# Last MLP, gates, selection and experts in one stage: four batches at a time, outputs added up in two PSUM banks

## The chip, the cores and the metric

The kernel runs on one core of a Trainium2 chip. The metric is the device time of one execution in microseconds (us); the median of three runs is given. The work is done by five engines with queues of their own: TensorE (PE, matmuls into PSUM), VectorE (DVE), ScalarE (ACT), GpSimd (POOL) and SyncE (SP, which issues the DMAs here).

## The reference

The network is a chain of eight blocks on `x` of 16 batches x 256 tokens x 128 features: four times an attention (or a scan) and a feed-forward block, each with a layer norm ahead of it and one on its output, and a residual addition. Only the end matters here: the last MLP of the block `L3_attn`, and the block `L3_ffn`, a mixture of experts in which each expert chooses its tokens.

```python
xa = xa + a_mlp_scale * (jnp.square(relu(rms_norm(xa) @ a_fc_w)) @ a_proj_w)   # last MLP
x = x + _layernorm(xa)
# L3_ffn on _layernorm(x): 8 experts, k = 64 tokens for each of them in each batch
probs = softmax(x @ gate_w).transpose(0, 2, 1)
g, m = top_k(probs, 64)
h = gelu(einsum('nekd,edf->nekf', x[m], w1)); h = einsum('nekf,efd->nekd', h, w2)
out = zeros.at[m].add(g[..., None] * h)            # scattered back to the tokens, bfloat16
x = x + _layernorm(out)
```

(The program text has `n` = 4 and `t` = 512 as constants, but takes both from the shape of `x`: 16 batches of 256 tokens, `k` = 64.)

## The kernel before

The 16 batches are held as eight groups `x[g]` of two batches, 128 tokens on the partitions, `[128, 4, 128]`, in float32. The program (L1778) is a row of stages. Each opens a pool for its work tiles on the left side of SBUF and its own PSUM pool; weights lie in pools on the left or right. All DMAs are issued from SP. A stage is written as Python generators, one for each group or unit, that `yield` between steps; `interleave` (L218) runs at most `depth` of them at a time and starts the next when the one before has made `lead` steps; `turns` (L372) starts each generator at a turn given for it. This sets the order in which instructions are written down. Where a stage isn't under `manual_schedule` (the attention and scan stages are), a scheduler then reorders the instructions of each engine and gives out the buffers of each tag as they come free. At run time each engine takes its instructions in the order so fixed, and waits on semaphores.

The end of the program is two stages:

- `stage_l3_last` (L1632), depth 4 and lead 2: for each of the eight groups the last MLP (`l3_mlp`, L1426: RMS norm, four transposes, four up matmuls of 512 columns, square of the ReLU on ACT and DVE, sixteen down matmuls), the residual with a layer norm (`residual`, L280; the statistics on DVE, the power -0.5 on POOL at L244), and `choice_gate` (L1645: layer norm into `exn`, four transposes, the gate's four matmuls of 8 columns, softmax over 8 experts with Exp on ACT at L1662, probabilities written to `probs` by POOL at L1668).
- `stage_choice_moe` (L1671): one selection for all 16 x 8 = 128 rows (batch, expert) of 256 probabilities: two transposes, then eight times the eight largest (`max`) and their replacement (`match_replace`) on DVE, the mask of the chosen, transposes back, three matmuls for the rank of each chosen token, `slot`. Then `pair_of(half, pair)`, for each half (eight batches) and each pair of experts, at depth 2: for each batch a one-hot matrix `hot` (DVE, L1722) and the same times the probabilities, `back` (POOL, L1724); a matmul gathers the tokens with `hot`; a transpose of `back` makes `put`; four up matmuls of 512 columns and a Gelu for each expert (L1744); down matmuls, 32 for each four batches (two experts side by side in the array); the outputs are copied to `y`. `put` and `y` of all four pairs are kept (6 buffers each). Behind the last pair of a half, for each group, 16 matmuls add up `put` x `y` over the four pairs in one PSUM bank; then `ob` (bfloat16), the layer norm, the addition on POOL and the output DMA.

PSUM in both stages is four tags of two banks: `BANKS = {"mm": 2, "s": 2, "o": 2, "t": 2}`. `copy` (L232) gives copies to DVE and ACT by turns. The pools around it: the l3 weights `wc` on the left (opened L1856), the experts' weights `wd` on the right (L1873).

Of the kernel before, what the change touches and what calls it, by code (L numbers as in the profile page):

```python
# [24 lines left out]
AF = mybir.ActivationFunctionType  # L25
ALU = mybir.AluOpType
# [1399 lines left out]
def l3_mlp(k, x, fc, proj, bufs=3):  # L1426

    n = yield from k.rmsnorm(x, "n", 3)
    yield
    nT = k.transposed(n, "nT", 3)  # L1430
    yield
    h = k.t([P, 4, GT], "mlp_h", 3)
    for i in range(4):
        ps = k.ps("s")
        k.mm(ps, fc[:, i * P : (i + 1) * P], nT)
        r = k.t([P, GT], "mlp_r", bufs)
        k.nc.scalar.activation(r, ps, AF.Relu)
# [191 lines left out]
        k.turns(items + [(at[-1] - 5, rotate())])  # L1629


def stage_l3_last(k, x, xm, w, rows, then):  # L1632


    def last(g):
        yield from l3_mlp(k, xm[g], w["afc"], w["aproj"])
        yield
        yield from k.residual(x[g], xm[g])
        yield
        yield from then(g)  # L1640

    k.interleave([last(g) for g in range(NG)], 4, 2)


def choice_gate(k, x, g, w, xn, probs):  # L1645


# [20 lines left out]
        nc.gpsimd.tensor_copy(probs[:, :, at : at + ne], p[:, 2 * b : 2 * b + 2, :])  # L1668


def stage_choice_moe(k, x, w, xn, probs, out):  # L1671

    nc, v = k.nc, k.nc.vector
    ident, ones = k.c["ident"], k.c["ones"]
    ne, cap = 8, 64

    ps = k.ps("t")
    for t in range(2):  # L1680
        nc.tensor.transpose(ps[:, t * P : (t + 1) * P], probs[:, t, :], ident)  # L1681
    cur = k.t([P, SEQ], "top", 2)
    v.tensor_copy(cur, ps[:, :SEQ])
    for _ in range(cap // 8):
        best = k.t([P, 8], "best", 2)
        v.max(out=best, in_=cur)
        nxt = k.t([P, SEQ], "top", 2)
        v.match_replace(out=nxt, in_to_replace=best, in_values=cur, imm_value=-1.0)
        cur = nxt
    chosen = k.t([P, SEQ], "chosen", 1)  # L1690
    v.tensor_scalar(chosen, cur, 0.0, None, ALU.is_lt)
    ps = k.ps("t")
    for t in range(2):
        nc.tensor.transpose(ps[:, t * P : (t + 1) * P], chosen[:, t * P : (t + 1) * P], ident)  # L1694
    mk = k.t([P, 2, P], "mk", 1)
    v.tensor_copy(mk, ps[:, :SEQ].rearrange("p (t r) -> p t r", t=2))

    rank = k.ps("s")[:, :SEQ].rearrange("p (t r) -> p t r", t=2)
    k.mm(rank[:, 0, :], k.c["before"], mk[:, 0, :])
    k.mm(rank[:, 1, :], ones, mk[:, 0, :], True, False)  # L1700
    k.mm(rank[:, 1, :], k.c["before"], mk[:, 1, :], False, True)
    slot = k.t([P, 2, P], "slot", 1)
    v.scalar_tensor_tensor(slot, rank, 1.0, mk, ALU.add, ALU.mult)
    v.tensor_scalar(slot, slot, -1.0, None, ALU.add)


    iota = k.c["iota"].rearrange("p (e c) -> p e c", e=2)
    puts, ys = {}, {}

    def pair_of(half, pair):  # L1710
        b0 = 8 * half
        put = puts[half, pair] = k.t([P, 8, SEQ], "put", 6)
        y = ys[half, pair] = k.t([P, 8, D], "ey", 6)
        xinT = k.t([P, 8, P], "xinT", 2)
        for i0 in range(0, 8, 4):
            xin = k.ps("o").rearrange("p (b c) -> p b c", b=4)
            for i in range(i0, i0 + 4):
                b = b0 + i
                r = b * ne + 2 * pair
                hot = k.t([P, 2, P], "hot", 4)  # L1720
                by_expert = hot.rearrange("p t (e c) -> p t e c", e=2)
                v.tensor_tensor(by_expert, bc(iota, 1, 2), bc(slot[:, :, r : r + 2], 3, cap), ALU.is_equal)  # L1722
                back = k.t([P, 2, P], "back", 4)
                nc.gpsimd.tensor_tensor(  # L1724
                    back.rearrange("p t (e c) -> p t e c", e=2), by_expert, bc(probs[:, :, r : r + 2], 3, cap), ALU.mult
                )
                for t in range(2):
                    k.mm(xin[:, i - i0, :], xn[b // 2][:, 2 * (b % 2) + t, :], hot[:, t, :], t == 0, t == 1)
                tp = k.ps("t")
                for t in range(2):  # L1730
                    nc.tensor.transpose(tp[:, t * P : (t + 1) * P], back[:, t, :], ident)  # L1731
                k.copy(put[:, i, :], tp[:, :SEQ])
                if i % 2:
                    yield
            k.copy(xinT[:, i0 : i0 + 4, :], xin)
        yield
        hs = []
        for j in range(2):
            w1 = w[f"w1_{2 * pair + j}"]
            h = k.t([P, 4, GT], "mlp_h", 3)  # L1740
            for f in range(4):
                ps = k.ps("s")
                k.mm(ps, w1[:, f * P : (f + 1) * P], xinT[:, :, j * cap : (j + 1) * cap])
                nc.scalar.activation(h[:, f, :], ps, AF.Gelu_apprx_tanh)  # L1744
                if f % 2:
                    yield
            hs.append(h)
        for i0 in range(0, 8, 4):
            ps = k.ps("mm").rearrange("p (b d) -> p b d", b=4)
            for i in range(i0, i0 + 4):  # L1750
                for f in range(4):
                    for j in range(2):
                        rows = slice(j * cap, (j + 1) * cap)
                        w2 = w[f"w2_{2 * pair + j}"].rearrange("p (c n) -> p c n", c=4)
                        k.mm(ps[rows, i - i0, :], hs[j][:, f, i * cap : (i + 1) * cap], w2[:, f, :], f == 0, f == 3)
            k.copy(y[:, i0 : i0 + 4, :], ps)
            yield
        if pair < 3:
            return
        for g in range(b0 // 2, b0 // 2 + 4):  # L1760
            ps = k.ps("o").rearrange("p (t d) -> p t d", t=NT)
            for n in range(NT):
                i, t = 2 * g + n // 2 - b0, n % 2
                for p in range(4):
                    k.mm(
                        ps[:, n, :], puts[half, p][:, i, t * P : (t + 1) * P], ys[half, p][:, i, :], p == 0, p == 3
                    )
            ob = k.t([P, NT, D], "ob", 3, dt=BF16)
            nc.scalar.copy(ob, ps)
            yield  # L1770
            yield from k.residual(x[g], ob)
            nc.sync.dma_start(out=out[2 * g : 2 * g + 2].rearrange("b (t p) d -> p (b t) d", p=P), in_=x[g])

    k.interleave([pair_of(half, pair) for half in range(2) for pair in range(4)], 2, 6)


@with_exitstack
def program(ctx: ExitStack, tc: tile.TileContext, xin, dram, at, out):  # L1778
    nc = tc.nc
# [42 lines left out]
    k = Ctx(tc, const, None, None)  # L1822
# [42 lines left out]
    with pool("first", "left") as pf:  # L1865
        first = []
        stage("l3m", "left", stage_trunk, l2, rows1["l2b2"], l3, rows3, lm, xm, first, pf, banks=MAMBA_BANKS)
        closed("lm")
        closed("wb")
        with phase("l3g", RING_BANKS):  # L1870
            l3_gqa(k, xm, l3, l3["gain"], first)

    pd = opened("wd", "right")  # L1873
    moe = load(pd, "moe")
# [5 lines left out]
    closed("wc")  # L1880
    stage("l3f", "left", stage_choice_moe, moe, en, probs, out)
    closed("wd")

# [19 lines left out]
```

## Time and profile before

| | |
|---|---|
| median of 3 runs | 3027.43 us (3027.18 to 3029.25) |
| the profiled execution's own time | 3030.76 us |
| its span, first to last instruction | 3029.1 us |
| busy: PE / DVE / ACT / POOL | 2758.7 / 1984.5 / 1602.5 / 1013.6 us |
| mean granted clock of TensorE | 0.956 |
| last MLP and gates (stage `l3q`) | 2689 to 2809.6 us |
| selection | 2809.6 to 2822.9 us |
| experts, first gather to last down matmul | 2822.9 to about 3004.5 us |
| last sums, norms and output | to 3029.1 us |

Lines of the profile name an engine, a line of the code, an operation, and the tiles written and read. L316 is the helper of all matmuls, so there the tile tells which one it is. "PEclk" is the share of full speed that TensorE's clock was granted. In the chain of work that ended last each line is a start in us, a duration in us, an engine and what it did, with the number of records; "issue" is time in which an engine waited for nothing that the profile shows.

### The profile page before, as it was taken

How to read it: one execution, taken by the hardware profiler on the slowest of the kernel's cores; microseconds unless marked ns; L12 is line 12 of the kernel's file. 1: busy time of each engine (PE TensorE's matmuls, PEld its weight loads, DVE VectorE, ACT ScalarE, POOL GpSimd, SP SyncE). 2: the span in 40 equal slices, each digit the busy share in tenths (PEclk: the TensorE clock that was granted, in tenths of full speed). 3: DMA queues.
4: the chain of work that ended last, by engine and by line, in shares of the span. 5: the costliest groups of instructions: out<-in, count | busy, mean ns of one | idle time of the engine just before them, and what ended most of it. 6: DMA issues, size and time to landing. Idle time of an engine off the chain costs nothing. (4 is left out here: it accounts for less than half of the span.)

```text
span 3029.1 us, 59064 instructions
## 1 busy us (share of the span) xinstructions
PE 2758.7 (91%) x23516; PEld 1855.1 (61%) x23516; DVE 1984.5 (66%) x5375; ACT 1602.5 (53%) x3372; POOL 1013.6 (33%) x1368
## 2 busy tenths in 40 slices
PE   8879999999997799999959997899999699978798
PEld 4547766767765588888834443566666344435576
DVE  5667465574657899999676773666655677637432
ACT  6745556455563577777615664444443377632222
POOL 3553333333336100000044553322322466553232
PEclk9989999999998899999979998999999799988899
DMA  4000000000000000000010000000000000010000
GB/s 114 11 1 2 1 2 2 1 2 1 2 5 33 4 12 8 8 8 9 19 62 1 1 2 1 1 2 1 1 1 2 1 1 1 2 56 1 1 15 15
DMA packets 29147, 31.26 MB, mean 10 GB/s; under 512 B 7292, under 2 KB 20156, under 8 KB 28732
## 3 DMA queue, kind: packets, MB, share of 16 engines
q1 hardware_dynamic: 28872, 27.49, 3.0%
q8 instruction: 185, 3.03, 0.4%
q14 instruction: 90, 0.74, 0.1%
HBM read 23.29 MB, written 4.19 MB: 9 GB/s over the span
## 5 line engine op out<-in xcount | busy, mean ns | idle before, releaser
L243 POOL TENSOR_SCALAR ln_rs<-ln_mv 128x4 f32<-128x4 f32 x192 | 39.8, 207 | 858.3 <-DVE ln_mv L256 836.8
L439 DVE TENSOR_REDUCE at_nm<-ps_s 128x2 f32<-128x512 f32 (+1 forms) x384 | 238.3, 682 | 124.2 <-PE ps_s L316 124.2
L471 ACT ACTIVATE at_e<-ps_s 128x512 f32<-128x512 f32 x384 | 198.2, 603 | 93.2 <-PE ps_s L316 91.1
L1390 DVE TENSOR_TENSOR scan<-ps_s,lm 128x384 f32<-128x384 f32 x256 | 124.8, 550 | 143.1 <-PE ps_s L316 142.8
L477 POOL TENSOR_SCALAR_AFFINE_SELECT at_e<-at_e 128x1024 f32<-128x1024 f32 (+1 forms) x96 | 135.4, 1411 | 215.5 <-ACT at_e L471 215.2
L244 POOL TENSOR_TENSOR ln_rs<-ln_rs,mhalf 128x4 f32<-128x4 f32 x192 | 195.8, 1020 | 15.7
L853 DVE TENSOR_REDUCE l_max<-ps_s 128x3 f32<-128x384 f32 x256 | 124.1, 549 | 64.0 <-PE ps_s L316 64.0
L316 PE MATMUL ps_o<-my,meT 128*128 128x129 f32 x1024 | 145.5, 289 | 18.4 <-ACT mgot L1147 15.4
L316 PEld LDWEIGHTS ps_s<-l_w,mlp_h 128*128 128x128 f32 x1280 | 149.4, 192 | 18.8 <-issue 15.1
L316 PE MATMUL ps_s<-l1f_phi,mxT 128*128 128x256 f32 x512 | 141.4, 398 | 16.9 <-DVE mpart L1009 16.7
L316 PE MATMUL ps_s<-km,qT 32*128 32x512 f32 x768 | 141.5, 666 | 11.9 <-POOL km L363 10.5
L316 PEld LDWEIGHTS ps_o<-my,meT 128*128 128x128 f32 x1024 | 128.6, 196 | 37.1 <-ACT mgot L1147 21.9
L316 PE MATMUL ps_s<-l_w,mlp_h 128*128 128x128 f32 x1280 | 150.2, 275 | 0.3
L316 PE MATMUL ps_s<-qm,kT 32*128 32x512 f32 x768 | 143.4, 652 | 5.2 <-DVE at_nm L439 5.0
L903 POOL TENSOR_SCALAR_AFFINE_SELECT e<-e 128x512 f32<-128x512 f32 x128 | 78.8, 637 | 178.3 <-ACT e L900 178.3
L316 PE MATMUL ps_o<-at_e,at_vm 128*32 128x128 f32 (+1 forms) x2048 | 123.4, 338 | 15.3 <-ACT at_oT L501 15.3
L316 PE MATMUL ps_mm<-mdisp,mxn 128*128 128x128 f32 x1024 | 125.2, 278 | 5.0 <-DVE mdisp L1047 4.9
L316 PEld LDWEIGHTS ps_mm<-mdisp,mxn 128*128 128x128 f32 x1024 | 121.7, 195 | 7.9 <-DVE mdisp L1047 6.6
L900 ACT ACTIVATE e<-ps_s 128x384 f32<-128x384 f32 x256 | 105.5, 510 | 39.7 <-PE ps_s L316 39.6
L316 PE MATMUL ps_s<-xT,l_w 128*128 128x512 f32 x256 | 119.3, 596 | 2.7 <-ACT mlp_h L788 2.7
L1367 ACT COPY BT<-ps_s 128x512 f32<-128x512 f32 x64 | 37.5, 586 | 154.6 <-PE ps_s L316 154.6
L316 PEld LDWEIGHTS <-b_ident 128*128 128x128 bf16 x656 | 51.3, 98 | 110.1 <-issue 100.0
(428 smaller groups left out, 7040.8 us busy)
## 6 DMA issues: line engine op xcount, KB each, us to landing
mw<-in_l1fw SPq DMA_DIRECT2D x16, 256.0 KB, 2.6
moe_w<-in_moe SPq DMA_DIRECT2D x16, 256.0 KB, 5.3
l_w<-in_l SPq DMA_DIRECT2D x10, 256.0 KB, 3.1
x<-in_x SPq DMA_DIRECT2D x8, 256.0 KB, 4.4
xs<-x SPq DMA_DIRECT2D x8, 256.0 KB, 2.0
slT<-xs SPq DMA_DIRECT2D x8, 256.0 KB, 2.6
out<-x SPq DMA_DIRECT2D x8, 256.0 KB, 2.3
l1f_phi<-in_l1f SPq DMA_DIRECT2D x1, 1024.0 KB, 5.0
```

Source lines behind the costliest of these rows:

```text
L243: g.tensor_scalar(out, in_, scale, eps, ALU.mult, ALU.add)
L244: g.tensor_tensor(out, out, self.mhalf[:, :n], ALU.pow)
L316: self.nc.tensor.matmul(out, lhsT=lhsT, rhs=rhs, start=start, stop=stop, skip_group_check=True)
L439: v_.tensor_reduce(nm[:, t, r, vs], s, AX.X, ALU.max, negate=True)
L471: nc.scalar.activation(e[:, r], s, AF.Exp)
L477: nc.gpsimd.affine_select(at, at, [[0, 4], [0, n], [1, P]], ALU.is_ge, 0.0, base=0, channel_multiplier=-1)
L853: v.tensor_reduce(mx[:, b, :, h, 16], s, AX.X, ALU.max, negate=True)
L900: nc.scalar.activation(e[:, h].rearrange("p j n -> p (j n)"), s[:, : 3 * P], AF.Exp)
L903: nc.gpsimd.affine_select(e[:, :, j, :], e[:, :, j, :], [[0, 4], [1, P]], ALU.is_ge, 0.0, base=0, channel_multiplier=-1)
L1367: nc.scalar.copy(s, ps)
L1390: v.tensor_tensor(m, s[:, : SEQ + P], lm[:, SCAN_HEADS[4 * (t // 2) + 2 * i + hh], :], ALU.mult)
```

## The change

The two stages become one, `stage_last`, which starts its generators by turns:

- `last(g)`: MLP, residual and gate of a group, as before, started every two turns for the first six groups, the last two at turns 16 and 20;
- `selection(q)`, q = 0 to 3: the selection of one quarter (four batches, 32 rows of 256), at turns 15, 19, 23 and 36;
- `pair_of(q, pair)`: one pair of experts for four batches, one every three turns from turn 21. An up matmul has 256 columns instead of 512, two of them share a bank and a Gelu. The outputs of a pair are added at once, in eight matmuls, into two PSUM banks that stay open over the four pairs (`sums`, one bank for each of the quarter's two groups), so `put` and `y` of a pair are free after it (4 and 3 buffers).

PSUM becomes one ring of six banks for everything, and two for the sums. `mlp_r` in the MLP has 2 buffers instead of 3. The l3 weights go to the right side, the two of the last MLP (`afc`, `aproj`) in a pool of their own, loaded first; the l2 weights' pool `wb` stays open to the end.

In the changed program the instructions of each engine stand as before up to the start of the l2 attention, where VectorE's casts of `att_sel` and `att_rows` come before the first norm instead of after the first maxima; from there they are equal up to the last stage. On SP the l3 weights, which stood behind the eight reloads `slT<-xs` of the soft stage, stand between them. In the last stage ScalarE has five table loads (Gelu, Exp, Gelu, Exp, Gelu), where it had one: the gates of the last two groups stand between Gelus. TensorE and VectorE stand so, in outline:

```
TensorE: MLP of groups 0 to 5, gates 0 to 4 and selection 0 among them; MLP of group 6;
  gathers of (0,0) with the up matmuls of group 7; selection 1; (0,0) with gathers of (0,1); gate 6;
  sums of (0,0); gathers of (0,2); selection 2; ... then one (q, pair) after the other
VectorE: MLP, norms and gates of groups 0 to 4, nearly all of 5, n and mlp_h of 6; selection 0;
  four hot; selection 1, group 6; four hot; selection 2, group 7; hot of (0,2) ...
```

The diff (`-` and `+`; its core):

```diff
+LAST_BANKS = {"s": 6, "sum": 2, "mm": "s", "t": "s"}
...
-    k.interleave([last(g) for g in range(NG)], 4, 2)
...
-def stage_choice_moe(k, x, w, xn, probs, out):
+def stage_last(k, x, xm, w, xn, probs, out):
...
+    def last(g):
+        yield from l3_mlp(k, xm[g], w["afc"], w["aproj"], 2)
+        yield
+        yield from k.residual(x[g], xm[g])
+        yield
+        yield from choice_gate(k, x, g, w, xn, probs)
+
+    def selection(q):
+        rows = nb * ne
+        ps = k.ps("s")
+        for t in range(2):
+            nc.tensor.transpose(ps[:rows, t * P : (t + 1) * P], probs[:, t, rows * q : rows * (q + 1)], ident)
+        cur = k.t([rows, SEQ], "top", 2)
+        v.tensor_copy(cur, ps[:rows, :SEQ])
+        for n in range(cap // 8):
+            best = k.t([rows, 8], "best", 2)
+            v.max(out=best, in_=cur)
+            nxt = k.t([rows, SEQ], "top", 2)
+            v.match_replace(out=nxt, in_to_replace=best, in_values=cur, imm_value=-1.0)
+            cur = nxt
+            if n % 2:
+                yield
...
-    def pair_of(half, pair):
-        b0 = 8 * half
-        put = puts[half, pair] = k.t([P, 8, SEQ], "put", 6)
-        y = ys[half, pair] = k.t([P, 8, D], "ey", 6)
-        xinT = k.t([P, 8, P], "xinT", 2)
+    def pair_of(q, pair):
+        put = k.t([P, nb, SEQ], "put", 4)
+        y = k.t([P, nb, D], "ey", 3)
+        xinT = k.t([P, nb, P], "xinT", 2)
...
+        h = k.t([P, 2, 4, SEQ], "mlp_h", 3)
         for j in range(2):
             w1 = w[f"w1_{2 * pair + j}"]
+            for f in (0, 2):
+                ps = k.ps("s")
+                for u in range(2):
+                    at = (f + u) * P
+                    k.mm(ps[:, u * SEQ : (u + 1) * SEQ], w1[:, at : at + P], xinT[:, :, j * cap : (j + 1) * cap])
+                nc.scalar.activation(
+                    h[:, j, f : f + 2, :], ps.rearrange("p (u n) -> p u n", u=2), AF.Gelu_apprx_tanh
+                )
+            yield
...
+        if pair == 0:
+            sums[q] = [k.ps("sum").rearrange("p (t d) -> p t d", t=NT) for _ in range(2)]
+        for u, o in enumerate(sums[q]):
+            for n in range(NT):
+                i, t = 2 * u + n // 2, n % 2
+                k.mm(o[:, n, :], put[:, i, t * P : (t + 1) * P], y[:, i, :], pair == 0 and n == 0, pair == 3)
         if pair < 3:
             return
...
-    k.interleave([pair_of(half, pair) for half in range(2) for pair in range(4)], 2, 6)
+    items = [(2 * g if g < 6 else 4 * g - 8, last(g)) for g in range(NG)]
+    for q in range(4):
+        items.append(((15, 19, 23, 36)[q], selection(q)))
+        items += [(21 + 12 * q + 3 * pair, pair_of(q, pair)) for pair in range(4)]
+    k.turns(items)
...
-    pc = opened("wc", "left")
-    l3 = load(pc, "l3")
+    pe = opened("we", "right")
+    last = load(pe, "l3", {"afc", "aproj"})
+    pc = opened("wc", "right")
+    l3 = load(pc, "l3", set(at["l3"]) - set(last))
+    l3.update(last)
...
-    gate = lambda g: choice_gate(k, x, g, moe, en, probs)
-    stage("l3q", "left", stage_l3_last, xm, l3, rows3, gate)
+    stage("last", "left", stage_last, xm, last, en, probs, out, banks=LAST_BANKS)
...
-    stage("l3f", "left", stage_choice_moe, moe, en, probs, out)
```

More of the change, by code (lines that the diff above doesn't have):

```diff
@@ L1629, in stage_trunk @@
         k.turns(items + [(at[-1] - 5, rotate())])
[L1632 to L1640, printed above, removed]
-    k.interleave([last(g) for g in range(NG)], 4, 2)
 def choice_gate(k, x, g, w, xn, probs):
@@ L1668, in choice_gate @@
         nc.gpsimd.tensor_copy(probs[:, :, at : at + ne], p[:, 2 * b : 2 * b + 2, :])
-def stage_choice_moe(k, x, w, xn, probs, out):
+def stage_last(k, x, xm, w, xn, probs, out):
     nc, v = k.nc, k.nc.vector
     ident, ones = k.c["ident"], k.c["ones"]
[L1677 to L1704, printed above, removed]
-    iota = k.c["iota"].rearrange("p (e c) -> p e c", e=2)
-    puts, ys = {}, {}
-    def pair_of(half, pair):
-        b0 = 8 * half
-        put = puts[half, pair] = k.t([P, 8, SEQ], "put", 6)
-        y = ys[half, pair] = k.t([P, 8, D], "ey", 6)
-        xinT = k.t([P, 8, P], "xinT", 2)
[L1715 to L1735, printed above, removed]
-        yield
-        hs = []
@@ new lines, in stage_last @@
+    ne, cap, nb = 8, 64, 4
+    iota = k.c["iota"].rearrange("p (e c) -> p e c", e=2)
+    slots, sums = {}, {}
+    def last(g):
+        yield from l3_mlp(k, xm[g], w["afc"], w["aproj"], 2)
+        yield
+        yield from k.residual(x[g], xm[g])
[16 more added lines that the diff above has]
+                yield
+        chosen = k.t([rows, SEQ], "chosen", 1)
+        v.tensor_scalar(chosen, cur, 0.0, None, ALU.is_lt)
+        ps = k.ps("s")
+        for t in range(2):
+            nc.tensor.transpose(ps[:, t * rows : (t + 1) * rows], chosen[:, t * P : (t + 1) * P], ident[:rows, :rows])
+        mk = k.t([P, 2, rows], "mk", 2)
+        v.tensor_copy(mk, ps[:, : 2 * rows].rearrange("p (t r) -> p t r", t=2))
+        rank = k.ps("s")[:, : 2 * rows].rearrange("p (t r) -> p t r", t=2)
+        k.mm(rank[:, 0, :], k.c["before"], mk[:, 0, :])
+        k.mm(rank[:, 1, :], ones, mk[:, 0, :], True, False)
+        k.mm(rank[:, 1, :], k.c["before"], mk[:, 1, :], False, True)
+        slot = slots[q] = k.t([P, 2, rows], "slot", 3)
+        v.scalar_tensor_tensor(slot, rank, 1.0, mk, ALU.add, ALU.mult)
+        v.tensor_scalar(slot, slot, -1.0, None, ALU.add)
+        yield
@@ new lines, in pair_of @@
+    def pair_of(q, pair):
+        put = k.t([P, nb, SEQ], "put", 4)
+        y = k.t([P, nb, D], "ey", 3)
+        xinT = k.t([P, nb, P], "xinT", 2)
+        xin = k.ps("s").rearrange("p (b c) -> p b c", b=nb)
+        for i in range(nb):
+            b, r = nb * q + i, i * ne + 2 * pair
+            hot = k.t([P, 2, P], "hot", 4)
+            by_expert = hot.rearrange("p t (e c) -> p t e c", e=2)
+            v.tensor_tensor(by_expert, bc(iota, 1, 2), bc(slots[q][:, :, r : r + 2], 3, cap), ALU.is_equal)
+            back = k.t([P, 2, P], "back", 4)
+            at = b * ne + 2 * pair
+            nc.gpsimd.tensor_tensor(
+                back.rearrange("p t (e c) -> p t e c", e=2), by_expert, bc(probs[:, :, at : at + 2], 3, cap), ALU.mult
+            )
+            for t in range(2):
+                k.mm(xin[:, i, :], xn[b // 2][:, 2 * (b % 2) + t, :], hot[:, t, :], t == 0, t == 1)
+            tp = k.ps("s")
+            for t in range(2):
+                nc.tensor.transpose(tp[:, t * P : (t + 1) * P], back[:, t, :], ident)
+            k.copy(put[:, i, :], tp[:, :SEQ])
+            if i % 2:
+                yield
+        k.copy(xinT, xin)
+        yield
+        h = k.t([P, 2, 4, SEQ], "mlp_h", 3)
@@ L1738, in pair_of @@
         for j in range(2):
             w1 = w[f"w1_{2 * pair + j}"]
-            h = k.t([P, 4, GT], "mlp_h", 3)
-            for f in range(4):
[L1742 to L1757, printed above, removed]
+            for f in (0, 2):
+                ps = k.ps("s")
+                for u in range(2):
[3 more added lines that the diff above has]
+                    h[:, j, f : f + 2, :], ps.rearrange("p (u n) -> p u n", u=2), AF.Gelu_apprx_tanh
+                )
@@ new lines, in pair_of @@
+            yield
+        ps = k.ps("s").rearrange("p (b d) -> p b d", b=nb)
+        for i in range(nb):
+            for f in range(4):
+                for j in range(2):
+                    rows = slice(j * cap, (j + 1) * cap)
+                    w2 = w[f"w2_{2 * pair + j}"].rearrange("p (c n) -> p c n", c=4)
+                    k.mm(ps[rows, i, :], h[:, j, f, i * cap : (i + 1) * cap], w2[:, f, :], f == 0, f == 3)
+        k.copy(y, ps)
+        yield
+        if pair == 0:
+            sums[q] = [k.ps("sum").rearrange("p (t d) -> p t d", t=NT) for _ in range(2)]
@@ L1758, in pair_of @@
+        for u, o in enumerate(sums[q]):
+            for n in range(NT):
+                i, t = 2 * u + n // 2, n % 2
+                k.mm(o[:, n, :], put[:, i, t * P : (t + 1) * P], y[:, i, :], pair == 0 and n == 0, pair == 3)
         if pair < 3:
             return
[L1760 to L1767, printed above, removed]
+        for u, o in enumerate(sums[q]):
+            g = 2 * q + u
@@ L1768, in pair_of @@
             ob = k.t([P, NT, D], "ob", 3, dt=BF16)
-            nc.scalar.copy(ob, ps)
+            nc.scalar.copy(ob, o)
             yield
@@ L1868, in program @@
         closed("lm")
-        closed("wb")
         with phase("l3g", RING_BANKS):
             l3_gqa(k, xm, l3, l3["gain"], first)
+    closed("wc")
     pd = opened("wd", "right")
-    moe = load(pd, "moe")
+    last.update(load(pd, "moe"))
     en = [pd.tile([P, NT, D], F32, tag=f"exn{g}", name=f"exn{g}") for g in range(NG)]
     probs = pd.tile([P, 2, NB * 8], F32, tag="probs", name="probs")
-    gate = lambda g: choice_gate(k, x, g, moe, en, probs)
-    stage("l3q", "left", stage_l3_last, xm, l3, rows3, gate)
+    stage("last", "left", stage_last, xm, last, en, probs, out, banks=LAST_BANKS)
+    closed("wd")
+    closed("we")
+    closed("wb")
     closed("xm")
-    closed("wc")
-    stage("l3f", "left", stage_choice_moe, moe, en, probs, out)
-    closed("wd")
 def kernel(**inputs):
```

## The prediction

> **What bounds the kernel now.** I read the page's slices first, to see which stretch the change touches; then the windows view by stage; then the chain of work that ended last; then the costliest groups by form for that stretch.
>
> ```profile
> PE   8879999999997799999959997899999699978798
> ...
> DVE  5667465574657899999676773666655677637432
> ...
> PEclk9989999999998899999979998999999799988899
> ```
>
> Slice 36 onwards (a slice is 75.7 us) is the part from 2689 us to the end: TensorE falls to 7 and 8 where its neighbours have 9. The windows view cuts this part by stage (last MLP, selection, experts, tail), then the MLP stage more finely:
>
> ```profile
> core 0: us, PE busy (x) PEld busy (x) DVE busy (x) ACT busy (x) POOL busy (x), PEclk, DMA share, GB/s
> 2689.00:2809.60 120.60, 87.94 (x448) 61.63 (x448) 80.33 (x296) 25.20 (x48) 52.77 (x81) 0.83 0.10 35
> 2809.60:2822.90 13.30, 3.00 (x10) 1.93 (x10) 9.18 (x30) 0.00 (x0) 0.08 (x1) 0.50 0.00 1
> 2822.90:3008.40 185.50, 182.22 (x1698) 142.55 (x1699) 65.16 (x160) 62.58 (x118) 51.11 (x76) 0.98 0.03 7
> 3008.40:3029.10 20.70, 10.66 (x96) 10.47 (x94) 8.79 (x48) 2.33 (x4) 9.91 (x12) 0.81 0.18 51
> ...
> 2710.00:2742.50 32.50, 28.51 (x168) 20.73 (x167) 24.25 (x86) 8.47 (x15) 12.03 (x16) 1.00 0.00 1
> 2742.50:2759.00 16.50, 12.46 (x46) 7.47 (x44) 10.95 (x51) 3.31 (x7) 5.56 (x11) 0.69 0.00 1
> 2793.20:2809.60 16.40, 7.26 (x34) 5.83 (x32) 9.61 (x53) 1.27 (x4) 6.14 (x15) 0.59 0.00 0
> ```
>
> The experts are TensorE's (182 of 185.5 us at clock 0.98). The MLP stage is nobody's: TensorE 88 of 121 us, part of it at a low clock, VectorE 80. The selection is one VectorE chain with everything else idle. The chain gives TensorE's unit prices:
>
> ```profile
> 2810.42 8.82 issue
> ...
> 2847.53 3.64 PE ps_mm L316 x64
> 2851.18 3.73 PE ps_s L316 x8
> ...
> 2867.49 3.64 PE ps_mm L316 x64
> ...
> 2918.36 3.57 PE ps_o L316 x32
> ```
>
> The code's 32 down matmuls are x64 here: a float32 matmul leaves two records. One pair of experts for eight batches repeats every 2867.49 - 2847.53 = 19.96 us; the sums of one group over four pairs are 3.57 us. Experts in all: 8 x 19.96 + 8 x 3.57 = 188.2 us. The MLP of one group at full clock: 4 up matmuls 3.44, 16 down 3.52, 8 transposes at 0.11, gate 0.96: 8.8 us, 70.3 for eight. With 1.6 for the selection TensorE has 260 us of work; it runs from 2695.3 (first transpose) to 3019.1 (last sum), 323.8 us. So 64 us are lost: 44 in the MLP stage, 12 in the selection, 7 among the experts. The first 6 us (the stage's first norms) and the last 10 (3019.1 to 3029.1) lie outside.
>
> **The change part by part.**
>
> *TensorE's own work* hardly moves. Expert matmuls with 512 columns become twice as many with 256; copies, Gelus (still 512 elements), gathers, down matmuls and sums are as many as before. Per quarter and pair: 9.98 + 1.79 = 11.8 us, times 16 = 188.3. Four selections of 32 rows for one of 128: the same 1.6 us cut in four, up to 1 us more in small matmuls.
>
> *VectorE gains three selections.* One of 128 rows has 9.18 us of VectorE in its window. Four of 32 rows cost as much in all if an operation's time goes with its rows, four times as much if with the 256 elements of a row. The nearest row is ScalarE's: a copy of 32x512 took 570 ns (L660), one of 128x512 586 (L238). So rows don't count, and I take +27.5 us (bounds 0 and 27.5). VectorE goes from 163.5 us (sum of the four stages) to 191 over some 325: free on average, not in the first third.
>
> *Where the end is set.* The order of the changed kernel's instructions has the first gather of pair 0 behind nearly six groups' MLP and the first selection on VectorE, and the second and third selection before pair 2's gather. From that gather on TensorE has more to do than anyone. So: when is VectorE there?
> Until 2742.5 both kernels do the same (four groups' MLP, one gate); I take that time over. VectorE's work up to pair 2's gather, by rows: 80.33 / 8 = 10.0 us a group; all eight groups less what comes later for groups 6 and 7 (about 4), so 76; selections 1 and 2 whole, 3 all but its end: 26.4; ten one-hots at 0.58, four copies at 0.42, one at 0.69: 8.2. Together 111. Done by 2742.5: 35.2 busy us since 2690 plus some 2.5 pulled forward. Left: 73.6 us. TensorE's content there is 87.3 - 31.4 = 56 us, so VectorE sets the pace. How dense can it run? In 2710 to 2742.5 it was busy 24.25 / 32.5 = 0.75, with TensorE at 0.88 and setting the pace itself. Now TensorE has slack and a third of the work is selection, which waits for no one inside: I take 0.87 (between 0.75 and 0.95). 73.6 / 0.87 = 84.6: pair 2's gather at 2827.
>
> *From there TensorE:* rest of pair 1 7.3, fourteen more at 11.8 = 164.8, last gate and selections 3.2: 175.3 us. The fourth selection's transpose stands in TensorE's queue with some 15 us of expert work between it and its start, about what VectorE then has queued (12): nothing. The sums wait for the copy of the experts' output with 0.86 us of matmuls between: nothing.
>
> *Table loads, a rule against this change.* Interleaving Exp (gates) with Gelu adds four loads by the order.
>
> ```profile
> L1744 ACT ACT_TABLE_LOAD x1 | 1.3, 1283 | 0.0
> ```
>
> The row gives 4 x 1.28 = 5.1 us on ScalarE, with no gap around the load (the Gelu starts 1.29 us after it). The Trainium skill, "ScalarE: Activation LUTs", What ACT_TABLE_LOAD costs, counts a drain of 1380 ns on top, 2.66 us a switch, and says to batch by set: 10.6 us. The row decides. ScalarE is busy 25 and 34% of these stages; behind the loads wait two Gelus each, and for them the down matmuls. One switch falls where VectorE paces, the other later: I charge 2 us (0 to 5).
>
> *The clock.* The skill, "TensorE: Matmul & The Clock Gate", What's actually happening, drops the clock to half after an idle window of about 3.4 us. In 2742.5 to 2759 no gap is longer than 1.5 us, and yet the row says 0.69. By the rule the 56 us of TensorE's content stay 56; by the row they become 81, just under VectorE's 84.6. The sum stands either way, but the slack is gone by the row.
>
> *Tail.* The last quarter ends with two groups at once where before groups came 3.6 us apart. After the last sum: copy, statistics, power, normalisation and add for one group (x at +5.0), then power, normalisation and add for the next (0.28 + 1.02 + 1.12 + 1.27): +8.8, and 3.4 from the last add to the end as now. 12.2 against 10.0.
>
> *Loads and pools.* The l3 weights move to the other side and are queued between the soft stage's eight reloads on SP; a reload behind them may land 4 us later (1.25 MB at the 4 MB in 13 us of 2690), but the last is issued at 1538.9 and its add runs at 1554.7: covered. At the next attention's start VectorE's casts of the attention rows now stand ahead of the first norm, which ran at 1561.0; issued at 1556 with 2.0 to 2.6 us to land they are there: 0 (at most +2; -2 if the freed queue helps). Expert weights load from 2690 as before and are first needed 90 us on.
>
> **Sum.** 2742.5 + 84.6 + 175.3 + 2 + 12.2 = 3016.6 us span. The profiled execution took 3030.76 (span 3029.1); the median 3027.43 is 1.7 below that span. So 3014.9, say 3015: 12 us, 0.4%. Of the 64 lost us most come back as VectorE's wait.
>
> **Rivals.**
> *TensorE is fed all along.* If VectorE's queue hides well, TensorE needs its 56 us at the 0.88 of 2710 to 2742.5: 64 us, gather at 2806. Then 2806 + 177.3 + 12.2 - 1.7 = 2994. For it: no bubble of four groups in flight any more (2742.5 to 2759). Against: VectorE's 73.6 us are more than 64 even without any gap, unless I over-counted.
> *Coupling as before.* VectorE no denser than the 0.75 the trace shows: 98.7 us, gather at 2841, 3029: no change. For it: in-order queues and POOL's power (1.0 us a norm) remain.
> *Half clock, slower.* TensorE, starved from 2742.5 to pair 2, runs at 0.5 as in the selection's window. Its 56 us become 112, it decides once the clock is under 56 / 84.6 = 0.66; gather at 2855 or later: 3042.
>
> **Numbers.** VectorE-paced 0.50 (3008 to 3022 for 0.95 to 0.80), fed 0.20 (2990 to 3000), coupling 0.22 (3023 to 3031), half clock 0.08. Some 0.2% (6 us, to 3021.4) is what a measurement of this kernel can tell from no change: faster 0.69, same 0.23, slower 0.08. The range 2993 to 3030 leaves out the half-clock case and the quicker part of the fed one.
>
> **What would show it.** VectorE over 0.85 busy between 2743 and 2825 with TensorE near 0.65; pair 2's gather near 2827; from there TensorE unbroken for some 177 us; five Gelu and Exp loads of 1.28 us; 12 us after the last sum; nothing before 2689 moved by over 2 us. It is wrong if VectorE idles much there, if TensorE stalls in the experts' steady part, or if an earlier stage moves.

## The result, and the profile after

The changed kernel takes 3016.59 us (median of 7 runs, 3013.64 to 3021.05), the kernel before on the same chip 3029.03 (7 runs): ratio 0.9966, 95% interval 0.9954 to 0.9977. The profiled execution took 3016.38 us, its span is 3014.7.

The slices, as they answer to those of before:

```profile
PE   8979999999997799999959997899999699978898
...
DVE  5667465574657989999776774565765577638542
...
PEclk9989999999998899999979998899999799988999
```

Counted from 0, slice 37, which held the selection, has an 8 for TensorE and a 9 for its clock instead of 7 and 8; VectorE has 8, 5, 4 in slices 36 to 38 instead of 7, 4, 3. What happened inside is read from the stage's own beginning, the first square of the RMS norm on GpSimd. It stands at 2685.8 us here and stood at 2690.3 in the trace of before, so 4.5 of the 14.4 us between the two spans (3029.1 and 3014.7) come from ahead of the stage. From that instruction to the end, the **stage** took 338.8 us before and takes 328.9: 9.9 us less. The windows of the changed kernel, cut at the points that the prediction speaks of (52.2 us after the beginning, which is 2742.5 in the trace of before; the gather of pair (0,2); the last sum):

```profile
core 0: us, PE busy (x) PEld busy (x) DVE busy (x) ACT busy (x) POOL busy (x), PEclk, DMA share, GB/s
2685.80:2738.00 52.20, 38.14 (x187) 26.55 (x188) 35.40 (x99) 11.69 (x20) 27.94 (x37) 0.84 0.23 81
2738.00:2823.90 85.90, 67.60 (x424) 55.10 (x423) 71.09 (x294) 22.14 (x40) 31.54 (x54) 0.84 0.00 1
2823.90:3002.80 178.90, 176.90 (x1799) 163.79 (x1797) 67.73 (x206) 61.12 (x113) 48.04 (x72) 1.00 0.04 10
3002.80:3014.70 11.90, 0.00 (x0) 0.00 (x0) 4.14 (x24) 0.58 (x1) 4.94 (x6) 0.72 0.15 44
```

All four rows are near the forecast: the first 52 us as before (38.1 us of TensorE, 35.4 of VectorE), then 85.9 us up to the gather, then TensorE almost without a break at full clock (176.9 of 178.9 us), then a tail of 12. Where TensorE stands in the second row, its timeline tells (start, duration, and in brackets how long it was idle before and who ended that):

```profile
2762.77 1.61 PE L306 MATMUL ps_s<-const_ident,exn 128*128 128x128 f32 x3 [4.17 <-DVE exn L264]
2766.18 3.47 PE L317 MATMUL ps_s<-nT,l_afc 128*128 128x512 f32 x4 [1.15 <-DVE nT L237]
...
2770.30 1.96 PE L317 MATMUL ps_s<-nT,l_afc 128*128 128x512 f32 x4
2775.40 0.31 PE L1697 MATMUL ps_s<-const_ident,chosen 32*128 32x32 f32 x2 [3.15 <-DVE chosen L1694]
...
2778.59 5.78 PE L317 MATMUL ps_s<-l_aproj,mlp_h 128*128 128x128 f32 x32
...
2795.51 0.28 PE L1697 MATMUL ps_s<-const_ident,chosen 32*128 32x32 f32 x2 [3.77 <-DVE chosen L1694]
...
2818.70 3.78 PE L317 MATMUL ps_sum<-ey,put 128*128 128x128 f32 x16 [4.17 <-DVE ey L237]
...
2823.91 0.61 PE L317 MATMUL ps_s<-hot,exn 128*128 128x128 f32 x4
```

TensorE waits for a norm, for selection 0, for selection 1 and for a copy, 3 to 4 us each time and each time for VectorE, whose queue holds selections, norms and MLP of several groups in turn. The last line is the gather of pair (0,2). Behind such a wait the clock is low: the same four up matmuls take 3.47 us at 2766 and 1.96 at 2770. VectorE is not busy all of the time either: of its 14.8 idle us in this stretch, the profile puts 5.8 down to waits for GpSimd (the powers and additions of the norms) and 2.7 to waits for ScalarE.

### The profile page after: what moved, and what is told of

It reads as the page before. It is cut to its first block, busy times and chain, and to the rows that moved or that the text cites. A ratio compares the mean times of both kernels' runs of the same rounds, so it can differ in the third digit from the quotient of the medians.

```text
span 3014.7 us, 59480 instructions
## 1 busy us (share of the span) xinstructions
PE 2753.9 (91%) x23674; PEld 1882.7 (62%) x23674; DVE 1999.3 (66%) x5462; ACT 1607.1 (53%) x3376; POOL 1010.7 (34%) x1368
## 3 DMA queue, kind: packets, MB, share of 16 engines
q8 instruction: 187, 3.06, 0.4%
## 4 chain that ended last, share of the span: by engine, by line
PE 48%; DVE 9%; ACT 6%; POOL 3%; issue 2%; DMA 0%; POOLq 0%; SPq 0%; ACTq 0%; DVEq 0%
PE ps_s L317 30%; PE ps_o L317 7%; PE ps_mm L317 6%; ACT at_e L472 1%; ACT lg L1129 1%; PE ps_s L306 1%; POOL ln_rs L245 1%; ACT meT L1136 1%; PE ps_sum L317 1%; ACT mdisp L1036 1%; DVE ln_st L255 1%; ACT lg L1009 1%; PE ps_s L506 1%; PE ps_t L1134 1%; DVE at_nm L440 1%
## 5 line engine op out<-in xcount | busy, mean ns | idle before, releaser
L317 PE MATMUL ps_s<-km,qT 32*128 32x512 f32 x768 | 139.8, 659 | 11.9 <-POOL km L364 10.5
L317 PE MATMUL ps_o<-at_e,at_vm 128*32 128x128 f32 (+1 forms) x2048 | 122.7, 336 | 15.2 <-ACT at_oT L502 15.2
```

The lines of the kernel that those rows point to most:

```text
L317: self.nc.tensor.matmul(out, lhsT=lhsT, rhs=rhs, start=start, stop=stop, skip_group_check=True)
```

## The experiments

All are compared by two measures: the median with its ratio to the kernel before on the same chip, and the length of the stage in the profiled run, from its first instruction to the end. The second is the finer one, since the stage's beginning falls anywhere from 2685.8 to 2692.5 us in kernels built on the changed one, and from 2688.4 to 2694.8 in those built on the kernel before, though all of a family are equal up to it. Two runs of the changed kernel gave 328.9 us and the same gathers within 0.1 us. That is partly luck: in both, TensorE's clock went down and up again at the same times after the stage's beginning, to within 0.1 us (at half from 1.5, full from 15.1 or 15.2 us on). In the run with half the rounds in selection 3, every engine has the changed kernel's order up to 184 us, but the clock came back at 17.1 us; there the gather of (0,1) came 0.8 us later and that of (0,2) 1.0 us earlier. So a difference under some 2 us between two traces isn't read as an effect here. Each kernel has one trace, the changed one two; the medians are of 5 to 22 runs. "First gather" and "gather (0,2)" count from the stage's first instruction.

| kernel | median us | ratio to before (95%) | stage us | first gather | gather (0,2) |
|---|---|---|---|---|---|
| before | 3029.03 | 1 | 338.8 | 133.1 | |
| changed | 3016.59 | 0.9966 (0.9954 to 0.9977) | 328.9 | 99.7 | 138.1 |
| all squares on ScalarE | 3018.80 | 0.9974 (0.9966 to 0.9982) | 329.3 | 100.3 | 138.6 |
| half the rounds, selections 0 to 2 | 3009.46 | 0.9944 (0.9932 to 0.9957) | 318.2 | 95.8 | 128.7 |
| half the rounds, selection 3 | 3018.61 | 0.9974 (0.9963 to 0.9986) | 330.6 | 99.2 | 137.2 |
| an Exp in every pair | 3022.12 | 0.9983 (0.9977 to 0.9990) | 331.0 | 99.2 | 137.2 |
| changed, again | 3017.97 | 0.9964 (0.9952 to 0.9977) | 328.9 | 99.7 | 138.1 |
| squares of groups 5 to 7 on ScalarE | 3014.02 | 0.9947 (0.9935 to 0.9960) | 322.4 | 93.8 | 131.7 |
| two selections, the second late | 3016.55 | 0.9965 (0.9951 to 0.9978) | 327.7 | 99.0 | 127.5 |
| parts in a row | 3018.39 | 0.9968 (0.9955 to 0.9980) | 329.1 | 117.8 | 137.2 |
| before, groups by turns | 3018.14 | 0.9955 (0.9943 to 0.9968) | 322.8 | 117.8 | |
| two selections, the second early | 3013.52 | 0.9944 (0.9932 to 0.9957) | 321.0 | 103.4 | 134.1 |
| the same, late squares on ScalarE | 3012.31 | 0.9940 (0.9927 to 0.9954) | 319.2 | 101.8 | 132.2 |
| before by turns, late squares on ScalarE | 3019.48 | 0.9949 (0.9935 to 0.9962) | 328.5 | 122.0 | |

**Does VectorE pace the stretch before pair (0,2)?** Five kernels take work from VectorE or add it to ScalarE.

```diff
-        k.nc.vector.tensor_tensor(h[:, i, :], ps, r, ALU.mult)
+        k.nc.scalar.activation(h[:, i, :], r, AF.Square)
```

> The changed kernel with the MLP's square moved from VectorE to ScalarE: h = Square(r) instead of ps * r. Theory (VectorE paces TensorE from 2742.5 us to the gather of pair (0,2) at 2823.9): 13 of the 32 multiplications stand in that stretch, 0.60 us each from start to start; without them 7.8 us less of VectorE's work, at the density of 0.83 some 9 us: the gather near 2815, the time near 3007 us. Rival (the stretch is set by the way through the norms, GpSimd's power and TensorE at a low clock, and VectorE only looks full): VectorE idles instead, the time stays between 3013 and 3017.

Measured: the gather of (0,2) after 138.6 us, nothing gained. The rival's number, but not for its reason alone: the first groups' MLPs became slower. A run of 26 down matmuls that both orders have begins 58.0 us after the stage's beginning in the changed kernel (at 2743.80 us) and 61.7 here; of these 3.7 us, 3.2 were won back up to the gather.

```diff
-        for n in range(cap // 8):
+        for n in range(cap // 8 if q == 3 else cap // 16):
```

> The changed kernel with four rounds of max and replace instead of eight in the selections of quarters 0, 1 and 2: only 32 tokens for each expert are chosen there, and the other half of the slots stays empty; all later work has its full size. Theory (VectorE paces the stretch): each loses 4 x (0.34 + 0.07 + 0.40) = 3.3 us of VectorE, 9.8 in all, at 0.83 some 12 us: near 3005. Rival (chain of norms and clock): 3013 to 3017.

Measured: gather (0,2) 9.4 us earlier for 9.8 us of VectorE's work, stage 10.7 less.

```profile
2817.88 0.61 PE L317 MATMUL ps_s<-hot,exn 128*128 128x128 f32 x4
```

With the stage's beginning at 2689.15 that is 128.7 us, and no wait stands before it. VectorE's work there counts nearly one for one. Fewer rounds also make the selection's own chain shorter, so this run alone doesn't tell VectorE's work from that chain; the run with the late squares, below, does.

And for selection 3 alone:

```diff
-        for n in range(cap // 8):
+        for n in range(cap // 8 if q < 3 else cap // 16):
```

> The same cut in the selection of quarter 3 alone, which runs beside the experts (2865 to 2881 us): 32 tokens for each expert are chosen in quarter 3, all later work has its full size. Theory (there TensorE sets the pace and the selection is hidden): 0, at most 1 us, 3015 to 3017. Rival (VectorE's queue holds TensorE up there too, TensorE being 0.91 busy in 2870 to 2880): 2 to 3 us less.

Measured: stage 330.6, 1.7 us longer rather than shorter. Selection 3 is hidden behind the experts, as predicted: the 2 to 3 us less of the rival did not come. The 1.7 us more are within what traces of one order differ by, and the interval of the ratio holds the changed kernel's.

```diff
+            if j == 0:
+                e = k.t([P, 8], "spare", 2)
+                nc.scalar.activation(e, h[:, 0, 3, :8], AF.Exp)
```

> The changed kernel with an Exp of 8 columns (its result unused) between the two experts' Gelus of every pair: about 30 table loads more, most of them beside the experts. My prediction's charge (2 us for four loads): 0.5 us a load, +15 us, near 3032. The rule with the drain, 2.66 us each and none of it hidden: +80 us, near 3096. All hidden behind ScalarE's idle time: under 3 us, at most 3020.

Measured: 37 table loads instead of 5, by the groups of ScalarE in the stage (count | busy us, mean ns | idle before):

```profile
L1744 ACT ACT_TABLE_LOAD x19 | 24.4, 1283 | 0.3
L1750 ACT ACT_TABLE_LOAD x16 | 20.5, 1283 | 0.3
L1650 ACT ACT_TABLE_LOAD x2 | 2.6, 1283 | 2.9 <-DVE p L1649 2.9
```

The 32 loads more are 41 us of ScalarE, and the stage grew by 2.1: 0.07 us a load. Nearly all of it lies in ScalarE's idle time. (This profiled run began its stage at 2692.5, before any of the added instructions, so most of its span's excess isn't theirs. The median is 5.5 us over the changed kernel's, which was measured on another chip, and the intervals of the two ratios only touch: by the medians a load would cost 0.17 us.)

The changed kernel, without an edit:

> The changed kernel itself once more, on the chip of the three runs beside it. The last stage's first instruction came at 2685.8 us in its first profile and between 2687.1 and 2692.5 us in four kernels that are equal to it up to there; 2690.3 us in the kernel before. If the earlier start is the change's (the loads moved to the other side), it comes near 2686 again; if it is chance, anywhere from 2686 to 2692. The stage itself, 328.9 us from there, stays within 1 us.

Measured: the stage began at 2689.6, and took 328.9 us. So the early beginning of its first profile isn't the change's; it was chance.

```diff
-        yield from l3_mlp(k, xm[g], w["afc"], w["aproj"], 2)
+        yield from l3_mlp(k, xm[g], w["afc"], w["aproj"], 2, g >= 5)
```

(The new last argument puts the square on ScalarE, as in the first of these kernels.)

> The changed kernel with the square on ScalarE for groups 5, 6 and 7 alone, so that the first five groups' instructions stay as they were. Theory of the prediction (VectorE's total work at its density paces): 12 x 0.60 / 0.83 = 8.7 us less up to the gather of pair (0,2), which lies 138.1 us after the stage's first instruction in the changed kernel: near 129.5, and near 3008 us in all. Rival (only the chains of the selections and norms count, and the square lies in the MLP's own chain whichever engine has it): 135 to 139, 3013 to 3018.

Measured: gather (0,2) at 131.7, 6.4 us earlier for 7.2 us of squares; stage 322.4.

```profile
2821.68 0.61 PE L317 MATMUL ps_s<-hot,exn 128*128 128x128 f32 x4
```

(The stage began at 2690.03.) The MLP's own chain still has the squares here, on ScalarE; only VectorE's queue has lost them. So the theory holds, a little under its size, and the first experiment's failure lies with the early groups.

**Can selections be taken out of the stretch?** The 96 rows of quarters 1 to 3 in one selection cost VectorE no more than 32.

```diff
+    items += [(15, selection(0, 1)), (33, selection(1, 3))]
     for q in range(4):
-        items.append(((15, 19, 23, 36)[q], selection(q)))
-        items += [(21 + 12 * q + 3 * pair, pair_of(q, pair)) for pair in range(4)]
+        items += [(21 + 12 * q + 3 * pair + 5 * (q > 0), pair_of(q, pair)) for pair in range(4)]
```

(Not shown: `selection(q, n_q)` takes `n_q` quarters at a time. The pairs of quarters 1 to 3 start five turns later.)

> The changed kernel with two selections instead of four: quarter 0 alone (32 rows) as now, quarters 1 to 3 together (96 rows) behind the last gate. VectorE's time for a selection doesn't go with its rows, so two selections of some 8 us leave the stretch before pair (0,2). Theory (the selections' chains on VectorE pace, as the run with half the rounds showed: 9.3 us for 9.8): 12 to 16 us less, gather of (0,2) near 124 us after the stage's first instruction, 3001 to 3005 in all. Rival (the 96 rows come after the last gate, and TensorE stands still before pair (1,0) until they are chosen): the gain is given back there, 3010 or more, with a gap before the gathers of (1,0). Second rival (TensorE at a low clock and GpSimd's powers pace): 3012 to 3017.

Measured: gather (0,2) 10.7 and (0,3) 12.0 us earlier, but then 24.4 us to (1,0) where the changed kernel needs 11.4, and the next pair at 177.1, where that has it at 176.6. The rival: the gain was given back. VectorE's timeline of this kernel shows how:

```profile
2841.54 0.29 DVE L1694 TENSOR_SCALAR chosen<-top 96x256 f32<-96x256 f32 x1
2846.74 0.36 DVE L1699 COPY mk<-ps_s 128x192 f32<-128x192 f32 x1 [4.91 <-PE ps_s L1697]
...
2850.63 0.41 DVE L1722 TENSOR_TENSOR hot<-const_iota,slot 128x256 f32<-128x256 f32 x1
```

VectorE was done with choosing at 2841.8, but the transposes of `chosen` stood in TensorE's queue behind 64 records of down matmuls, and only when they were through (4.91 us) could the ranks and the one-hots of (1,0) follow.

The second attempt starts all MLPs every two turns and puts the second selection right behind the last gate:

```diff
-    items = [(2 * g if g < 6 else 4 * g - 8, last(g)) for g in range(NG)]
+    items = [(2 * g, last(g)) for g in range(NG)]
+    items += [(15, selection(0, 1)), (26, selection(1, 3))]
...
-        items.append(((15, 19, 23, 36)[q], selection(q)))
```

> The changed kernel with two selections (quarter 0; quarters 1 to 3 together, 96 rows), all groups' MLPs started every two turns, and the second selection right behind the last gate, ahead of pair (0,2) in the order, so that it is done before pair (1,0), where the run with two selections lost again what it had gained. Theory: gather of (0,2) near 128 us after the stage's first instruction, (1,0) near 153 instead of 165.5, and from there 163.4 us as in the changed kernel: 316 to 318, time near 3005. Rival (MLPs of groups 6 and 7 ahead of everything put the first gather back to 110 or later, and the gain is spent before it begins): 324 to 328, 3012 to 3016.

Measured: 321.0, between the two. (The 165.5 us of the expectation belong to the second gather of (1,0); the first is at 163.1 in the changed kernel.) Pair (1,0) is gathered 11.8 us after (0,3), so the stall is gone; but the first three pairs come 15.2 and 15.5 us apart instead of 11.8. By the order of the lines, gates 6 and 7 and the one-hots stand in one another's way, and the clock is low meanwhile (four gathers in 1.19 us, 0.61 at full clock); which of the two counts more was not tested:

```profile
2793.57 1.19 PE L317 MATMUL ps_s<-hot,exn 128*128 128x128 f32 x4 [1.88 <-DVE hot L1722]
...
2799.71 0.71 PE L317 MATMUL ps_s<-hot,exn 128*128 128x128 f32 x4 [1.38 <-DVE hot L1722]
2801.51 0.45 PE L1732 MATMUL ps_s<-const_ident,back 128*128 128x128 f32 x2 [1.09 <-POOL back L1725]
...
2816.64 0.42 PE L1682 MATMUL ps_s<-const_ident,probs 128*96 128x128 f32 x2 [2.42 <-POOL probs L1656]
```

To this the late squares are added (Square on ScalarE where `g >= 5`, as above):

> The same with the square on ScalarE for groups 5, 6 and 7. Theory (VectorE paces up to the first gathers, as the run with the late squares showed: 6.4 us for 7.2 us of work): 3 to 6 us less than the run beside it, 3000 to 3003. Rival (with a selection less, VectorE has slack and TensorE or the selection's chain paces): within 1 us of it.

Measured: 1.8 us less in the stage, between both and within what traces of one order differ by, so this run doesn't decide. Of the kernels that leave out no work it is the fastest by both measures (3012.31 us, 319.2 us of stage), but the intervals of all the ratios from 0.9940 to 0.9955 overlap.

**What brought the gain?** First the changed kernel with its overlap taken away:

```diff
-    items = [(2 * g if g < 6 else 4 * g - 8, last(g)) for g in range(NG)]
+    items = [(2 * g, last(g)) for g in range(NG)]
     for q in range(4):
-        items.append(((15, 19, 23, 36)[q], selection(q)))
-        items += [(21 + 12 * q + 3 * pair, pair_of(q, pair)) for pair in range(4)]
+        items.append((34 + 12 * q, selection(q)))
+        items += [(40 + 12 * q + 3 * pair, pair_of(q, pair)) for pair in range(4)]
```

> The changed kernel with its parts in a row: all groups' MLPs and gates from turn 0 on, then the selection of quarter 0, then its pairs; quarters, one ring and sums in two banks stay, and the selections of the later quarters run beside the experts. It takes the overlap of MLP and experts away alone. Theory (the gain is the overlap's): MLP stage to some 118 us after its start, selection 12, TensorE 191, tail 12: 333 us of stage, 4 us over the changed kernel, near 3021. Rival (the gain comes from the quarters and the two banks, the overlap brings nothing): within 1 us of the changed kernel, 329.

Measured: 329.1 us, the rival's number. The first gather comes 18 us later than in the changed kernel, the gather of (0,2) 1.0 us earlier. Its TensorE waits:

```profile
2785.40 1.15 PE L306 MATMUL ps_s<-const_ident,exn 128*128 128x128 f32 x4 [4.34 <-DVE exn L264]
...
2792.17 1.15 PE L306 MATMUL ps_s<-const_ident,exn 128*128 128x128 f32 x4 [2.16 <-DVE exn L264]
...
2804.96 0.39 PE L1697 MATMUL ps_s<-const_ident,chosen 32*128 32x32 f32 x2 [8.65 <-DVE chosen L1694]
```

Between 52.2 us after the beginning and the gather of (0,2), TensorE stood still for 18.3 us in the changed kernel (85.9 less 67.60) and for 20.2 in this one (84.9 less 64.68); but its 424 records there took 2.9 us longer in the changed kernel. The overlap cuts one wait of 8.65 us for one selection into pieces of some 4 us, for two selections, a norm and a copy, and nothing that can be measured is left of it.

Then one edit to the kernel before, without merge, quarters and banks:

```diff
-    k.interleave([last(g) for g in range(NG)], 4, 2)
+    k.turns([(2 * g, last(g)) for g in range(NG)])
```

> The kernel before with one edit: the eight groups of the last MLP's stage start by turns, one every two turns, instead of at most four at a time. Everything behind it (one selection of 128 rows, pairs for eight batches, sums at the end of a half) stays. In the run with the parts in a row the last gate's matmuls ended 105 us after the stage's first instruction, against 119 us in the kernel before. Theory (the limit of four groups cost those 14 us, and the merge, the quarters and the two banks on balance nothing or less): stage 338.8 - 14 = 325 us, time near 3014. Rival (the ring of six banks brought it, not the turns): 336 to 339, within 2 us of the kernel before.

Measured: stage 322.8, 16.0 us less than before and 6.1 less than the changed kernel, in one trace, that of the fastest of its five runs. (The last gate's matmuls end 102.3 us after the beginning here, 105.4 with the parts in a row and 117.5 in the kernel before, not the 119 of the expectation.) The medians don't separate this kernel from the changed one: ratio 0.9955, and the interval (0.9943 to 0.9968) holds both the changed kernel's ratio and the 16 us. The windows of the kernel before between 2742.5 us and its selection, and then of this kernel from the same time of its trace (54.1 us after its beginning instead of 52.2; VectorE has 178 instructions left there instead of 195), its selection, and its experts (columns as in the windows above):

```profile
2742.50:2809.60 67.10, 49.89 (x259) 35.69 (x257) 45.12 (x195) 14.35 (x29) 22.72 (x43) 0.82 0.00 1
```

```profile
2742.50:2792.60 50.10, 38.68 (x239) 30.39 (x237) 39.58 (x178) 11.38 (x24) 21.11 (x40) 0.86 0.00 1
2792.60:2806.20 13.60, 2.99 (x10) 1.92 (x10) 9.63 (x31) 0.00 (x0) 0.00 (x0) 0.50 0.00 1
2806.20:3001.20 195.00, 192.30 (x1792) 152.75 (x1792) 69.86 (x191) 64.28 (x120) 56.91 (x84) 0.98 0.03 8
```

```profile
2806.22 1.22 PE L316 MATMUL ps_o<-hot,exn 128*128 128x128 f32 x4 [1.30 <-DVE hot L1722]
```

VectorE went from 0.67 busy (45.12 of 67.10) to 0.79 (39.58 of 50.10); the one edit lets more groups be in flight. The selection takes 13.6 us at clock 0.50, and took 13.3. The first gather, the last line, comes at 117.8 us, as with the parts in a row. The equal sums hide two differences: there the gates end 3.1 us later, and the selection of one quarter, which needn't wait for the last group's probabilities, takes 3.1 us less after them. What the ring of six banks or the pools' new sides do by themselves was not parted. From that gather to the end this kernel needs 205.0 us, the one with quarters and two banks 211.3: 1.9 more in the tail, and 4.4 more before it (TensorE busy 195.2 us against 192.3).

Last, to the kernel before both edits, the turns and the late squares:

```diff
-    k.interleave([last(g) for g in range(NG)], 4, 2)
+    k.turns([(2 * g, last(g)) for g in range(NG)])
...
-        yield from l3_mlp(k, xm[g], w["afc"], w["aproj"])
+        yield from l3_mlp(k, xm[g], w["afc"], w["aproj"], late=g >= 5)
```

> The kernel before with its groups started by turns, and the square on ScalarE for groups 5, 6 and 7: the two edits that gained most by themselves, without the merge, the quarters and the two banks. With the turns alone the first gather comes 117.8 us after the stage's first instruction, the stage takes 322.8 us, and VectorE is 0.79 busy in the 50 us ahead of the selection. Theory (VectorE paces the late groups there too, as in the changed kernel, where 7.2 us of squares less brought 6.4): 3 to 6 us less, 317 to 320 us of stage. Rival (the last groups' chain of norms, powers and gates paces, with nothing beside it): 322 to 323.

Measured: neither. The stage took 328.5 us, and the first gather came 4.2 us later than with the turns alone. Of these, 1.7 us were there 21 us after the beginning, before any edited instruction and in the same order on every engine: the clock was at half from 18.5 to 21.9 us, and full there with the turns alone. At the end of its MLP stage TensorE waits 5.31 us for the last group's norm (the first line, of this run) instead of 2.17 (the second, of the turns alone):

```profile
2797.46 1.25 PE L305 MATMUL ps_t<-const_ident,exn 128*128 128x128 f32 x4 [5.31 <-DVE exn L263]
```

```profile
2787.00 1.15 PE L305 MATMUL ps_t<-const_ident,exn 128*128 128x128 f32 x4 [2.17 <-DVE exn L263]
```

Why that norm came later was not traced further. The profiled run was the slowest of five (3025.01 us, the fastest 3013.90), and the medians don't separate the two kernels. So no gain from the squares is seen here, and a loss isn't sure. That they had nothing to make room for, without selections in VectorE's queue, would explain it, and is not shown.

## Why the prediction was right, and where its account was not

**The time.** 3015 was forecast and 3016.59 measured; the range and the side hold. Counted from the stage's beginning the forecast was 326.3 us (3016.6 less 2690.3), and 328.9 came: 2.6 us too little. The early beginning of the first profiled run hides that, and was chance; "nothing before 2689 moved by over 2 us" failed for the same reason.

**Up to 2742.5 as before.** Right: TensorE's and VectorE's work in these 52.2 us was 38.05 and 35.20 us before and is 38.14 and 35.40.

**84.6 us to the gather of (0,2).** 85.9 measured, for 71.1 us of VectorE's work (73.6 forecast) at a density of 0.83 (0.87). (The terms of the forecast, as printed, give about 73 rather than 73.6.) That VectorE paces is shown: 9.8 us of rounds less brought 9.4, 7.2 us of squares less brought 6.4. So TensorE was not fed all along (that rival's gather was 2806), the density is nearer 0.87 than the coupling's 0.75, and the half clock did not carry the gather to 2855. Two of the prediction's own signs were missed: VectorE was to be over 0.85 busy there, and TensorE near 0.65, where it was 0.79 (67.6 of 85.9), since its records took longer at the low clock.

**27.5 us for three selections more.** Right in its reason, that rows don't count. By the groups of VectorE the rounds of four selections of 32 rows take

```profile
L1687 DVE MAX8 best<-top 32x8 f32<-32x256 f32 x32 | 13.0, 406 | 0.1
L1689 DVE MATCH_REPLACE8 top<-best,top 32x256 f32<-32x256 f32 x32 | 12.7, 397 | 0.0
```

where the one of 128 rows took 428 and 408 ns each. With their small steps 33.2 us against 9.3: 23.9 more.

**175.3 + 2 us from there.** 178.9 up to the last sum. The content was 1.6 us short (TensorE busy 176.9), and the 2 us for loads were too much: at 0.07 us a load, the four would cost 0.3, and at the 0.17 of the medians, 0.7. The rule of the Trainium skill ("ScalarE: Activation LUTs", What ACT_TABLE_LOAD costs), 2.66 us each, would have made 85 us of the 32 loads of the experiment if none were hidden; the row's 1.28 us stands against its 2.66, and both are prices on ScalarE, not the kernel's.

**The clock.** TensorE's content was to stay 56 us by the rule and become 81 by the row; it was 67.6, since the clock was at half for a part of it only: around the waits of 4.17 and 3.15 us, for instance, from 2759.0 to 2769.2 and from 2776.1 to 2782.9. As VectorE set the pace, this was mostly covered, but not all: between 2776.0 and 2785.6 the chain of work runs over TensorE at a low clock (the 32 down matmuls in 5.78 us; 26 of them took 3.06 at full clock). What a warm TensorE would bring there wasn't tried.

**Tail.** 12.2 forecast, 11.9 measured.

**Where the account failed.** The sum charged the change as one thing, and named the missing limit of four groups only as a point for a rival. The runs part it, with one trace for each: 16.0 us come from that limit alone; the merge, the quarters, the ring and the two banks, in a row, take 6.3 of them back (329.1 less 322.8); the overlap of MLP and experts, for which the stage was merged, returns 0.2, which is nothing that can be measured. The 6.3 are more than the 1 to 2 us by which traces of one order differ, but the intervals of the medians overlap. "Of the 64 lost us most come back as VectorE's wait" was right as a number, and it was the finding: the overlap brings VectorE three selections more in just the stretch in which VectorE paces. So the time was right for the whole, and the account silent on where it came from; a forecast for each part would have had to face that.

## What to carry to other kernels

Before two stages are merged to fill a bubble, lift the limit that makes the bubble in the stage itself: here one line gave at least as much as the merge. Overlap did not pay here, because the engine that paces the overlapped stretch got more work with it: an operation whose time doesn't go with its rows was cut into four. Putting it together again helped only where it was finished before its user. And measure a late stage from its own first instruction: that varied by 1 to 2 us with the clock, where the whole varied by several.

## What the runs showed of the hardware

- Runs of equal code reach the last stage up to 6.7 us apart (2685.8 to 2692.5 us). In the nine runs of the kernel before that shared a chip with the turns, the span goes with the mean granted clock: 3024.5 us at 0.960, 3033.1 at 0.954.
- In all fourteen traces the granted clock is 1.0 or 0.5 and nothing between, so a mean such as 0.69 is a mixture, and every stretch between two changes lasts a multiple of 3.41 us (10.2 and 6.8 above). Where the changes fall differs from run to run: after the stage's beginning the clock is full again from 15.1 or 15.2 us on in seven traces, from 16.0 in one and from 17.1 in six.
- The clock falls without a single long wait, too: in the run with the late squares four up matmuls took 3.78 us (1.96 at full clock) after waits of 2.17, 0.25, 0.26, 0.17 and 1.15 us within 6 us:

```profile
2768.95 3.78 PE L317 MATMUL ps_s<-nT,l_afc 128*128 128x512 f32 x4 [1.15 <-DVE nT L237]
```

- A table load among Gelus cost the kernel 0.07 us by the stage's length, and 0.17 by the medians, where ScalarE was a third busy, though it takes 1.28 us itself.
- `max` and `match_replace` over 256 elements took 406 and 397 ns for 32 rows, 428 and 408 for 128: a selection cut into four by rows cost 23.9 us more.
